# A second mixture of experts that adds its results into the output rows by scatter, in place of a table of results

## The chip, the cores and the metric

The kernel runs on one core of a Trainium2 chip. The metric is the device time of one execution in microseconds (us). The engines are PE (matrix products; PEld is its weight load), DVE (vector), ACT (scalar, activations), POOL (GpSimd) and SP (Sync). Each takes its instructions in program order. SP, ACT and POOL also issue DMAs; the indirect ones, which gather or scatter rows by a list of indices, are issued by POOL alone.

## The reference

Four layers act on `x`, 3125 rows of 256 numbers in fp32, with 50000 edges: a graph layer, a mixture of 8 experts (hidden size 1024), a second graph layer and a second mixture of 8 experts (hidden size 256). Each adds its result to `x`. The change is in the last:

```python
def _moe(tokens, router_w, w1, b1, w2, b2):
    logits = tokens.astype(jnp.float32) @ router_w.astype(jnp.float32).T
    probs = jax.nn.softmax(logits, axis=-1)
    rw, re = jax.lax.top_k(probs, TOP_K)                       # TOP_K = 2, 8 experts
    rw = rw / jnp.maximum(rw.sum(-1, keepdims=True), 1e-12)
    combine = jnp.zeros((N, E), tokens.dtype).at[jnp.arange(N)[:, None], re].set(rw)
    out = tokens
    for e in range(E):
        h = jax.nn.gelu(tokens @ w1[e] + b1[e], approximate=False)
        y = h @ w2[e] + b2[e]
        out = out + combine[:, e:e + 1] * y
    return out
...
x = x + _L1_ffn_ref(_layernorm(x, axis=-1)[None], ...)[0]
return x
```

So a row of the final output is `x`, plus its normed row (`out = tokens`), plus two weighted results of experts.

## The kernel before

`X` holds all rows in the on-chip memory, as 25 tiles of 128 rows (the last has 53). The tiles are split in two halves, 14 and 11 tiles (`HALVES`). In each mixture every expert gets a fixed room of places per half: 4 units of 128 places in the first half, 3 in the second (`UNITS`); tokens past that would go to extra sets, which a branch at the end runs only where they are needed.

The second graph layer runs in `to_the_end`. Its products (L1503) fill PE; `finish_tile` follows each tile, and at the end of every group of up to five tiles `score` norms the rows, adds the normed rows to `X` on POOL (`plus_normed`, L1421) and forms the router's logits. When the first half is complete, `route_steps` ranks the experts, gives every token two places (`r.at`) and two weights (`r.weight`), and calls `list_steps`, which turns the places around: for every place, which token to take (`take`) and which row of a result table to put the result into (`put`). It does that by one-hot products: `lane` and `col` are comparisons made on DVE, and PE multiplies them (L751) in parts of up to `r.part` tiles. A place that no token holds gets an index outside the table, and the scatter leaves it out. For the first half the rows themselves are sent to their places (`dispatch`, L1475), and the experts read them in blocks; for the second half POOL gathers the rows by `take` (L909).

`experts` then runs 16 sets, 8 experts for each half. Its order is written out by hand: instructions go to each engine in the order of the code. For one set PE does the first product (L949), ACT the activation into `hid` (L953), PE the transposes for the next set (`turn`, L925, copied by DVE at L926) and the second product, one unit of 128 places after the other (L962); DVE adds the bias (L967) and POOL scatters the unit into the half's result table `ytab` (L968), which was cleared to zeros far ahead, during the first mixture (`clear_steps`). `take` issues the gathers for later sets between these. The scatters of all sets go to different rows of a table, and `alone` declares that they need no order. Generators run beside the sets, one step in each `slot()`: `beside_third` makes the second half's lists, and `beside_fourth`, once all of the first half's sets are done, reads the first half's table back (`results`), adds the two weighted results of each row to `X` (`combine`, L998) and stores the rows to `out`. After the last set `combine_all` does the same for the second half.

Of the kernel before, what the change touches and what calls it, by code (L numbers as in the profile page):

```python
# [16 lines left out]
P = 128  # L17
D = 256
# [71 lines left out]
def gnn_ffn_kernel(ctx: ExitStack, tc: tile.TileContext, x, src_a, src_d, dst_d, dst_row,  # L90
# [134 lines left out]
    def clear(ytab):  # L225
        for _ in clear_steps(ytab):
            pass

    def tables(h, layer, by_place=False):

        rows = (FIXED[h] + XS * SX if by_place else HALVES[h][1] - HALVES[h][0]) * P
        return (dram.tile([rows, D], F32, name=f"xtab{layer}{h}{int(by_place)}"),
                dram.tile([2 * tokens(h), D], F32, name=f"ytab{layer}{h}{int(by_place)}"))
# [343 lines left out]
    class Routed:  # L577
# [4 lines left out]

        def __init__(self, by_place=False, part=T):
            self.by_place = by_place
            self.part = part
            self.done = False
            self.lists = {}
# [32 lines left out]
    def route_steps(r, rp, h, pl, layer, sc=None):  # L620
# [87 lines left out]
        yield from list_steps(r, rp, h, layer, 0, FIXED[h])  # L708
# [17 lines left out]
        r.weight_x = keep.tile([P, 2, n], F32, tag=f"weightx{layer}{h}", name="weight_x")  # L726
        nc.vector.scalar_tensor_tensor(r.weight_x, r.at, FIXED[h] * P - 0.5, r.weight, OP.is_gt, OP.mult)
        yield

    def list_steps(r, rp, h, layer, c0, c1):  # L730


        t0, t1 = HALVES[h]
        n = t1 - t0
        nl = c1 - c0
        ati = rp.tile([P, 2, n], I32, name="ati")
        nc.vector.tensor_copy(ati, r.at)
        qi = rp.tile([P, 2, n], I32, name="qi")
        nc.vector.tensor_scalar(qi, ati, P - 1, None, OP.bitwise_and)
        qb = rp.tile([P, 2, n, 2], BF16, name="qb")  # L740
        nc.vector.tensor_copy(qb, qi[:, :, :, None].to_broadcast([P, 2, n, 2]))
        nc.vector.tensor_scalar(qi, ati, 7, None, OP.arith_shift_right)
        cb = rp.tile([P, 2, n, 2], BF16, name="cb")
        nc.vector.tensor_scalar(cb, qi[:, :, :, None].to_broadcast([P, 2, n, 2]), -float(c0), None, OP.add)
        pt = bank([P, 2, nl], F32, "sa", 1)
        parts = [(i, a, b) for i in range(2) for a, b in groups(n, r.part)]
        made = []

        def count(i, a, b, lane, col):
            for t in range(a, b):  # L750
                nc.tensor.matmul(pt, lane[:, t - a, :], col[:, t - a], start=(i + t == 0), stop=(i + t == n))  # L751

        for i, a, b in parts:
            yield
            m = b - a
            lane = rp.tile([P, min(r.part, n), P], BF16, name="lane", bufs=2)
            nc.vector.tensor_tensor(in_pairs(lane[:, :m]), pairs(qb[:, i, a:b], P),
                                    in_pairs(iota_b[:, None, :].to_broadcast([P, m, P])), OP.is_equal)
            yield
            col = rp.tile([P, min(r.part, n), 2, nl], BF16, name="col", bufs=2)  # L760
            nc.vector.tensor_tensor(in_pairs(col[:, :m, 1, :]), pairs(cb[:, i, a:b], nl),
                                    in_pairs(iota_b[:, None, :nl].to_broadcast([P, m, nl])), OP.is_equal)
            nc.vector.tensor_tensor(in_pairs(col[:, :m, 0, :]), in_pairs(col[:, :m, 1, :]),
                                    tile1[:, a:b, None, :].to_broadcast([P, m, nl // 2, 2]), OP.mult)
            nc.vector.tensor_scalar(col[:, :m, 1, :], col[:, :m, 1, :], row2[:, i:i + 1], None, OP.mult)
            made.append((i, a, b, lane, col))
            if len(made) == 2:
                yield
                count(*made.pop(0))
        yield  # L770
        for one in made:
            count(*one)
            yield
        yield
        low = rp.tile([P, nl], F32, name="low")
        nc.vector.tensor_scalar(low, pt[:, 1, :], -float(2 * P), None, OP.add)
        which = rp.tile([P, nl], F32, name="which")
        nc.vector.scalar_tensor_tensor(which, pt[:, 0, :], float(2 * P), low, OP.mult, OP.add)
        put = keep.tile([P, nl], I32, tag=f"put{layer}{h}{c0}", name="put")
        take = keep.tile([P, nl], I32, tag=f"take{layer}{h}{c0}", name="take")  # L780
        whole = rp.tile([P, nl], I32, name="whole")
        nc.vector.tensor_scalar(whole, which, 0.0, None, OP.max)
        nc.vector.tensor_scalar(take, whole, 1, None, OP.arith_shift_right)
        none = rp.tile([P, nl], F32, name="no")
        nc.vector.tensor_scalar(none, pt[:, 0, :], 0.5, float(1 << 20), OP.is_lt, OP.mult)
        nc.vector.tensor_tensor(put, which, none, OP.max)
        r.lists[c0, c1] = (take, put)
        r.done = True
# [37 lines left out]
    def alone(dma, table, fresh=False):  # L826

        group = f"{table.name}{fresh}"
# [26 lines left out]
    def experts(fp, sets, routed, tabs, weights, nh, act, beside=(), fresh=False, early=0, loaded=None,  # L855
# [74 lines left out]
        with tc.manual_schedule(engines=ENGINES):  # L930
# [9 lines left out]
            for k, (h, e, x) in enumerate(sets):  # L940
# [16 lines left out]
                take(1)  # L957
                slot()
                for j in range(n):
                    py = bank([P, D], F32, "y")  # L960
                    for c in range(nh):
# [6 lines left out]
                    alone(nc.gpsimd.indirect_dma_start(  # L968
                        out=tabs[h][1], out_offset=bass.IndirectOffsetOnAxis(ap=routed[h].column(c0 + j)[1], axis=0),
                        in_=y, in_offset=None, bounds_check=2 * tokens(h) - 1, oob_is_err=False), tabs[h][1], fresh)  # L970
# [30 lines left out]
    def combine_all(fp, h, r, ytab, over, then=lambda t0, t1: None, bufs=2):  # L1001
        spans = groups(HALVES[h][1], 2, HALVES[h][0])
        ahead = []
        for i, (t0, t1) in enumerate(spans):
            while len(ahead) < min(bufs, len(spans) - i):
                ahead.append(results(fp, h, ytab, *spans[i + len(ahead)], bufs))
            y2 = ahead.pop(0)
            for t in range(t0, t1):
                combine(h, r.weight_x if over else r.weight, y2, t0, t)
            then(t0, t1)  # L1010

    def store(t0, t1):
        whole = min(t1, T - 1)
        if whole > t0:
            nc.sync.dma_start(out=out[t0 * P:whole * P, :].rearrange("(t p) d -> p t d", p=P),
                              in_=X[:, t0:whole, :])
        if t1 == T:
            nc.sync.dma_start(out=out[(T - 1) * P:, :], in_=X[:LAST, T - 1, :])
# [156 lines left out]
    with tc.tile_pool(name="ffn", bufs=2, reuse_waits="tile") as fp:  # L1175
# [134 lines left out]
        def beside_first():  # L1310
# [7 lines left out]
            with tc.tile_pool(name="onehots", bufs=2, reuse_waits="tile") as hp:  # L1318
                yield from total_in(hp, into)
                clears = [c for table in (tabs2[0][0], tabs2[0][1], tabs2[1][1]) for c in (clear_steps(table),)]  # L1320
                for i, _ in enumerate(count_edges(hp, 0, T)):
                    if i % 10 == 9 and clears and next(clears[0], 0) == 0:
                        clears.pop(0)
                    yield
                for c in clears:
                    for _ in c:
                        pass
# [94 lines left out]

    def to_the_end():


        routed2 = [Routed(True, 5), Routed()]
        with tc.tile_pool(name="ahead", bufs=6, side="right", reuse_waits="tile") as ap, \
# [18 lines left out]
            def finish_tile(sp, t, s):  # L1446
# [8 lines left out]
                if t == t1 - 1:  # L1455
                    unit(state["emb"], state["sq"], t0, t1)
                    h = int(t0 >= HALVES[1][0])
                    if t0 == HALVES[h][0]:
                        state["pl"] = bank([P, HALVES[h][1] - t0, NE], F32, "sb", 1)
                    score(sp, h, t0, t1, state["pl"], rWt, tabs2[h][0], plus_normed,  # L1460
                          state["kept"][:, t0:t1, :] if h == 0 else None, nc.scalar)
                    if h == 0 and t1 == HALVES[0][1]:
# [51 lines left out]
        with tc.tile_pool(name="ffn2", bufs=3, side="right", reuse_waits="tile") as fp:  # L1514
# [4 lines left out]
            def beside_fourth():  # L1519
                while now2[0] <= NE:  # L1520
                    yield
                with tc.tile_pool(name="behind", bufs=1, reuse_waits="tile") as zp:
                    spans = groups(HALVES[0][1], 2)
                    ahead = []
                    for i, (t0, t1) in enumerate(spans):
                        while len(ahead) < min(4, len(spans) - i):
                            ahead.append(results(zp, 0, tabs2[0][1], *spans[i + len(ahead)], 4))
                        if i == 0:
                            for _ in range(10):
                                yield  # L1530
                        y2 = ahead.pop(0)
                        for t in range(t0, t1):
                            combine(0, routed2[0].weight, y2, t0, t)
                            yield
                        store(t0, t1)
                        yield
                        yield

            now2 = [0]
            experts(fp, fixed(0) + fixed(1), routed2, tabs2, weights2, KD, AF.Gelu,  # L1540
                    [beside_third(), beside_fourth()], early=3, now=now2, room=24)
# [4 lines left out]
            with tc.tile_pool(name="last", bufs=1, reuse_waits="tile") as lp:  # L1546
                combine_all(lp, 1, routed2[1], tabs2[1][1], False, store, 6)
# [3 lines left out]
        with tc.If(more > 0):  # L1551
            with tc.tile_pool(name="ffn2", bufs=3, reuse_waits="tile") as fp:
                for h in range(2):
                    with tc.tile_pool(name="route4", bufs=1, reuse_waits="tile") as rp:
                        extra_sets(rp, h, routed2[h], 2)
                    experts(fp, extras_of(h), routed2, tabs2, weights2, KD, AF.Gelu, fresh=True)
                    combine_all(fp, h, routed2[h], tabs2[h][1], True, store)

    def to_the_end_by_edges():
# [162 lines left out]
        tabs2 = [tables(h, 2) for h in range(2)]  # L1722
        routed2 = []
        for h, (a, b) in enumerate(HALVES):
            with tc.tile_pool(name="score2", bufs=2, reuse_waits="tile") as sp, tc.tile_pool(name="route2", bufs=1, reuse_waits="tile") as rp:
                pl = bank([P, b - a, NE], F32, "sb", 1)
                for t0, t1 in groups(b, 5, a):
                    score(sp, h, t0, t1, pl, rWt, tabs2[h][0], plus_normed)
                routed2.append(route(rp, h, pl, 2))
                extra_sets(rp, h, routed2[h], 2)  # L1730
        with tc.tile_pool(name="ffn2", bufs=3, reuse_waits="tile") as fp:
            for h in range(2):
                clear(tabs2[h][1])
                experts(fp, fixed(h) + extras_of(h), routed2, tabs2, weights2, KD, AF.Gelu)
                combine_all(cp, h, routed2[h], tabs2[h][1], False, store)
# [59 lines left out]
```

## Time and profile before

| | |
|---|---|
| median of 14 runs | 1173.42 us (1169.17 to 1177.74) |
| the profiled execution | 1174.55 us, span 1172.8 us |
| PE busy | 1024.2 us (87%), PEld 765.1 us |
| DVE, ACT, POOL busy | 589.8, 323.6, 342.5 us |
| scatters into result tables (L968), both mixtures | 112, 1109 ns each on POOL |
| gathers of rows (L909), both mixtures | 80, 1019 ns each on POOL |
| weighting and adding results (L998), both mixtures | 100, 500 ns each on DVE |
| reads of result tables | 24 of 512 KB and 2 of 106 KB |

The times of the trace count from the span's start. The sets of the second mixture begin at about 998 us; the first graph layer, the first mixture and the second graph layer lie before. A row of a timeline gives the start, the time taken, the engine, the line with the operation, `out<-in`, and in brackets how long the engine was idle before it and what ended that.

### The profile page before, as it was taken

What the parts mean: (1) busy time and instruction counts of PE and PEld (TensorE: products, weight loads), DVE (VectorE), ACT (ScalarE), POOL (GpSimd) and SP (SyncE); (2) the same over time, 40 slices, a digit from 0 to 9 for tenths busy, and PEclk for the clock granted to TensorE, in tenths of its full rate; (3) what the DMA queues carried; (4) which work ended last, traced back from release to release, by engine and by line L of the source; (5) the groups of instructions that cost most, each with busy time, mean ns of one, the idle gap of its engine ahead of it and who ended that gap; (6) DMA issues with size and microseconds to landing.
All of it is one profiled execution on the core that took longest, in us unless ns stands there. A gap on an engine that the chain in (4) does not pass through costs nothing. (4 is left out here: it accounts for less than half of the span.)

```text
span 1172.8 us, 16050 instructions
## 1 busy us (share of the span) xinstructions
PE 1024.2 (87%) x6043; PEld 765.1 (65%) x6051; DVE 589.8 (50%) x1481; ACT 323.6 (28%) x709; POOL 342.5 (29%) x358
## 2 busy tenths in 40 slices
PE   6996455998999999999998999999999996877890
PEld 6984342666666677777666788888877785555660
DVE  9963383476365556565544162634371425722453
ACT  2362131121135555666432111121100112101110
POOL 1234506333332322222221111011122311366640
PEclk9787686999999999999998999999999996888895
DMA  7663254353247785786642170511122101754754
GB/s 211 222 175 106 77 185 122 120 174 109 86 112 250 269 281 206 273 295 211 216 159 94 68 272 3 225 56 57 57 88 69 50 28 58 223 163 143 259 188 158
DMA packets 116607, 179.41 MB, mean 153 GB/s; under 512 B 20204, under 2 KB 91237, under 8 KB 116393
## 3 DMA queue, kind: packets, MB, share of 16 engines
q1 hardware_dynamic: 94237, 120.40, 31.4%
q0 software_dynamic: 13296, 34.55, 9.0%
q10 hardware_dynamic: 8980, 23.26, 5.2%
q8 instruction: 51, 0.84, 0.3%
q14 instruction: 43, 0.35, 0.1%
HBM read 108.30 MB, written 71.76 MB: 154 GB/s over the span
## 5 line engine op out<-in xcount | busy, mean ns | idle before, releaser
L949 PE MATMUL big<-xs,w 128*128 128x512 f32 (+1 forms) x640 | 290.5, 580 | 15.9 <-ACT hid L953 13.4
L962 PE MATMUL y<-w,hid 128*128 128x256 f32 x1120 | 278.4, 394 | 17.8 <-ACT hid L953 10.1
L962 PEld LDWEIGHTS y<-w,hid 128*128 128x128 f32 x1120 | 207.1, 194 | 48.7 <-ACT hid L953 11.7
L1503 PEld LDWEIGHTS <-at 128*128 128x128 bf16 x1875 | 184.9, 99 | 29.8 <-DMA at<-atab 2.6
L968 POOL DMA_INDIRECT ytab<-y,put x112 | 124.2, 1109 | 228.8 <-DVE y L967 160.1
L953 ACT ACTIVATE hid<-big,bt 128x512 f32<-128x512 f32 (+1 forms) x160 | 101.6, 635 | 274.3 <-PE big L949 196.7
L949 PEld LDWEIGHTS big<-xs,w 128*128 128x128 f32 x640 | 116.7, 200 | 89.8 <-issue 43.8
L1503 PE MATMUL big<-parts,at 128*128 128x256 bf16 x1200 | 146.4, 275 | 2.1 <-DMA at<-atab 1.8
L909 POOL DMA_INDIRECT g<-xtab,take x80 | 81.5, 1019 | 174.3 <-PE tr L925 112.6
L967 DVE TENSOR_TENSOR y<-y,b2t 128x256 f32<-128x256 f32 x112 | 47.0, 423 | 135.6 <-PE y L962 112.3
L1160 PEld LDWEIGHTS <-hq 128*128 128x128 bf16 x800 | 57.2, 98 | 60.8 <-issue 40.4
L1140 DVE TENSOR_TENSOR hq<-qs,iota_b 128x2048 bf16<-128x2048 bf16 x50 | 61.1, 1222 | 54.0 <-PE sb L1160 46.1
L926 DVE COPY xs<-tr 128x512 f32<-128x512 f32 (+1 forms) x64 | 37.1, 619 | 74.6 <-PE tr L925 47.9
L998 DVE SCALAR_TENSOR_TENSOR X<-y,weight,X 128x256 f32<-128x256 f32 (+1 forms) x100 | 46.8, 500 | 46.6 <-DMA y<-ytab 45.6
L1503 PE MATMUL sa<-parts,at 128*128 128x256 bf16 x525 | 65.9, 277 | 1.6 <-issue 1.5
L1161 ACT CAST at<-sa 128x400 bf16<-128x400 f32 x100 | 49.1, 491 | 48.8 <-PE sa L1160 45.5
L1161 ACT CAST at<-sb 128x400 bf16<-128x400 f32 x100 | 49.1, 491 | 31.5 <-PE sb L1160 25.9
L1401 ACT COPY hT<-tr 128x512 f32<-128x512 f32 x25 | 14.4, 587 | 154.1 <-PE tr L1399 148.8
L1143 DVE TENSOR_TENSOR hc<-cs,iota_b 128x1600 bf16<-128x1600 bf16 x50 | 49.2, 985 | 0.0
L1421 POOL TENSOR_TENSOR X<-X,kept 128x256 f32<-128x256 f32 x14 | 10.4, 773 | 125.8 <-DVE kept L486 125.8
L519 PE MATMUL big<-gWo,hT 128*128 128x272 f32 x100 | 31.6, 456 | 16.6 <-remote 8.1
L417 PEld LDWEIGHTS <-hot 128*128 128x128 bf16 x391 | 40.6, 150 | 6.9 <-issue 3.8
(316 smaller groups left out, 1177.3 us busy)
## 6 DMA issues: line engine op xcount, KB each, us to landing
w<-in_fW SPq DMA_DIRECT2D x32, 1024.0 KB
atab<-at ACTq DMA_DIRECT2D x25, 800.0 KB
at<-atab SPq DMA_DIRECT2D x25, 800.0 KB
y<-ytab SPq DMA_DIRECT2D x24, 512.0 KB
ytab<-zero_b SPq DMA_DIRECT2D x10, 1024.0 KB
w<-in_mw SPq DMA_DIRECT2D x32, 256.0 KB
xtab<-zero_b SPq DMA_DIRECT2D x6, 1024.0 KB
rows<-xtab SPq DMA_DIRECT2D x8, 512.0 KB
```

The lines of the kernel that those rows point to most:

```text
L909: nc.gpsimd.indirect_dma_start(out=g, out_offset=None, in_=tabs[h][0], in_offset=bass.IndirectOffsetOnAxis(ap=routed[h].column(c)[0], axis=0))
L949: nc.tensor.matmul(ph[:, :n * P], w1[:, i, c * P:(c + 1) * P], turned[k][:, i, :n * P], start=(i == 0), stop=(i == KD - 1))
L953: nc.scalar.activation(hid[:, c, :n * P], ph[:, :n * P], act, bias=bt[:, 0, c:c + 1])
L962: nc.tensor.matmul(py, hid[:, c, j * P:(j + 1) * P], w2[:, c, :], start=(c == 0), stop=(c == nh - 1))
L967: nc.vector.tensor_add(y, py, b2t)
L968: alone(nc.gpsimd.indirect_dma_start(out=tabs[h][1], out_offset=bass.IndirectOffsetOnAxis(ap=routed[h].column(c0 + j)[1], axis=0), in_=y, ...
L998: nc.vector.scalar_tensor_tensor(X[:n, t, :], y2[:n, t - t0, i, :], weight[:n, i, i0:i0 + 1], X[:n, t, :], OP.mult, OP.add)
L1140: nc.vector.tensor_tensor(in_pairs(hq), pairs(qs[:, mine], P), in_pairs(iota_b[:, None, :].to_broadcast([P, n, P])), OP.is_equal)
L1143: nc.vector.tensor_tensor(in_pairs(hc), pairs(cs[:, mine], C), in_pairs(iota_b[:, None, :C].to_broadcast([P, n, C])), OP.is_equal)
L1160: nc.tensor.matmul(pa[:, j], hq[:, g + j, :], hc[:, g + j, :], start=True, stop=True)
L1161: nc.scalar.copy(at[:, :, W * (g0 + g):W * (g0 + g + 4)].rearrange("p i (g w) -> p i g w", w=W), pa.rearrange("p g i w -> p i g w"))
L1503: nc.tensor.matmul(sums[a][:, t - a, :], at[t][:, i, :], parts[:, i, k, :], start=False, stop=(i == T - 1 and k == 2 and t == b - 1))
```

## The change

The second mixture has no result table. Every tile of `X` is stored to `out` as soon as its normed rows have been added (`store` is called behind `score`, on ACT's queue). A unit's result is multiplied by the weights of its places on ACT and then scattered by an indirect DMA that adds to the rows of `out`. `list_steps` makes the weights by place: a weight is split in three bf16 parts, the one-hot columns are multiplied by each, and the same products sum them (`mine`). For this layer it therefore runs behind the weights in `route_steps`. A place that no token holds gets a row of the other half from an index fill (`spares`) and the weight 0, since the rows of one scatter have to differ. Scatters of one set are declared free of order among themselves, those of different sets no longer. `beside_fourth`, the last `combine_all` and the clears of two tables are gone; the first half's sets take one gather less each; the parts of the first half's list are 3 tiles long and not 5.

```diff
@@ route_steps
-        yield from list_steps(r, rp, h, layer, 0, FIXED[h])
+        if layer == 1:
+            yield from list_steps(r, rp, h, layer, 0, FIXED[h])
...
-        r.weight_x = keep.tile([P, 2, n], F32, tag=f"weightx{layer}{h}", name="weight_x")
-        nc.vector.scalar_tensor_tensor(r.weight_x, r.at, FIXED[h] * P - 0.5, r.weight, OP.is_gt, OP.mult)
+        if layer == 1:
+            r.weight_x = keep.tile([P, 2, n], F32, tag=f"weightx{h}", name="weight_x")
+            nc.vector.scalar_tensor_tensor(r.weight_x, r.at, FIXED[h] * P - 0.5, r.weight, OP.is_gt, OP.mult)
+        else:
+            yield from list_steps(r, rp, h, layer, 0, FIXED[h])
@@ list_steps
-        pt = bank([P, 2, nl], F32, "sa", 1)
+        kinds = 2 if layer == 1 else 5
+        if kinds > 2:
+            wb = rp.tile([P, 3, 2, n, 2], BF16, name="wb")
+            rest = r.weight
+            for k in range(3):
+                nc.vector.tensor_copy(wb[:, k], rest[:, :, :, None].to_broadcast([P, 2, n, 2]))
+                if k < 2:
+                    left = rp.tile([P, 2, n], F32, name="left", bufs=2)
+                    nc.vector.tensor_sub(left, rest, wb[:, k, :, :, 0])
+                    rest = left
+            yield
+        pt = bank([P, kinds, nl], F32, "sa", 1)
...
+            for k in range(2, kinds):
+                nc.vector.tensor_tensor(in_pairs(col[:, :m, k, :]), in_pairs(col[:, :m, 1, :]),
+                                        wb[:, k - 2, i, a:b, None, :].to_broadcast([P, m, nl // 2, 2]), OP.mult)
...
+            step = rp.tile([P, nl], F32, name="step")
+            spare = spares[h][:, c0:c1]
+            nc.vector.scalar_tensor_tensor(step, take, float(t0 * P), spare, OP.add, OP.subtract)
+            nc.vector.scalar_tensor_tensor(step, pt[:, 0, :], 0.5, step, OP.is_gt, OP.mult)
+            nc.vector.tensor_tensor(put, step, spare, OP.add)
+            mine = keep.tile([P, nl], F32, tag=f"mine{h}{c0}", name="mine")
+            nc.vector.tensor_reduce(mine, pt[:, 2:, :].rearrange("p k c -> p c k"), AX.X, OP.add)
+            r.lists[c0, c1] = (take, put, mine)
@@ experts
-                take(1)
+                if nh > 2 or h == 1:
+                    take(1)
...
-                    alone(nc.gpsimd.indirect_dma_start(
-                        out=tabs[h][1], out_offset=bass.IndirectOffsetOnAxis(ap=routed[h].column(c0 + j)[1], axis=0),
-                        in_=y, in_offset=None, bounds_check=2 * tokens(h) - 1, oob_is_err=False), tabs[h][1], fresh)
+                    to = routed[h].column(c0 + j)
+                    into = bass.IndirectOffsetOnAxis(ap=to[1], axis=0)
...
+                        nc.scalar.activation(y, y, AF.Identity, scale=to[2])
+                        alone(nc.gpsimd.indirect_dma_start(
+                            out=tabs[h][1], out_offset=into, in_=y, in_offset=None,
+                            bounds_check=N - 1, compute_op=OP.add), tabs[h][1], f"{h}{e}{x}")
@@ beside_first
-                clears = [c for table in (tabs2[0][0], tabs2[0][1], tabs2[1][1]) for c in (clear_steps(table),)]
+                clears = clear_steps(tabs2[0][0])
@@ to_the_end
+    spares = []
+
+    def spare_rows():
...
+            nc.gpsimd.iota(each[:, :FIXED[h]].rearrange("p (e u) -> p e u", e=NE), pattern=[[0, NE], [P, UNITS[h]]],
+                           base=base, channel_multiplier=1)
...
-        routed2 = [Routed(True, 5), Routed()]
+        routed2 = [Routed(True, 3), Routed()]
+        spare_rows()
...
                     score(sp, h, t0, t1, state["pl"], rWt, tabs2[h][0], plus_normed,
                           state["kept"][:, t0:t1, :] if h == 0 else None, nc.scalar)
+                    store(t0, t1, nc.scalar)
...
-            def beside_fourth():
...
             experts(fp, fixed(0) + fixed(1), routed2, tabs2, weights2, KD, AF.Gelu,
-                    [beside_third(), beside_fourth()], early=3, now=now2, room=24)
+                    [beside_third()], early=3, room=24)
...
-            with tc.tile_pool(name="last", bufs=1, reuse_waits="tile") as lp:
-                combine_all(lp, 1, routed2[1], tabs2[1][1], False, store, 6)
```

## The prediction

> **What bounds the kernel now.** I read the page first (engine rows, clock row, chain), then the chain of waits at its end, then tables by stage and the timelines of PE, POOL and DVE from 990 us on, and last the two built programs' orders. The page's second part says that PE is nearly full everywhere but at the start and in the last tenth:
>
> ```profile
> PE   6996455998999999999998999999999996877890
> ```
>
> The last zero is the stage that the change deletes. By stage (busy us of PE, PEld, DVE, ACT, POOL; then the granted clock, DMA share and GB/s):
>
> ```profile
> 1130.00:1145.00 15.00, 13.12 (x55) 9.42 (x53) 4.85 (x11) 2.33 (x4) 7.93 (x9) 1.00 0.15 57
> 1145.00:1173.00 28.00, 0.00 (x0) 0.00 (x0) 9.14 (x22) 0.00 (x0) 0.95 (x1) 0.52 0.49 160
> ```
>
> For 28 us no matmul runs. The chain of waits shows what does:
>
> ```profile
> 1144.96 2.31 DMA ytab<-y,put
> 1147.28 0.37 SPq L985
> 1147.70 2.64 SPq L985
> 1152.09 10.54 DMA y<-ytab
> 1162.72 0.49 DVE X L998
> ```
>
> The last scatter takes 2.31 us from issue to landing; then the second half's results are read back, combined (L998) and stored, and the span ends at 1172.8. From that landing to the end it is 25.5 us. The other engine that matters is POOL, which issues every scatter (L968) and gather (L909) in program order (start, us, tile):
>
> ```profile
> 1083.95 1.01 POOL L968 DMA_INDIRECT ytab<-y,put  x1 [4.85 <-DVE y L967]
> 1085.66 1.00 POOL L968 DMA_INDIRECT ytab<-y,put  x1 [0.69 <-DVE y L967]
> 1086.97 0.99 POOL L909 DMA_INDIRECT g<-xtab,take  x1 [0.30 <-issue]
> 1088.26 1.01 POOL L968 DMA_INDIRECT ytab<-y,put  x1 [0.30 <-issue]
> 1089.57 0.99 POOL L968 DMA_INDIRECT ytab<-y,put  x1 [0.30 <-issue]
> ...
> 1127.70 0.99 POOL L968 DMA_INDIRECT ytab<-y,put  x1 [0.30 <-issue]
> 1130.87 0.98 POOL L968 DMA_INDIRECT ytab<-y,put  x1 [2.18 <-DVE y L967]
> 1132.16 0.99 POOL L968 DMA_INDIRECT ytab<-y,put  x1 [0.30 <-issue]
> 1133.45 0.98 POOL L968 DMA_INDIRECT ytab<-y,put  x1 [0.30 <-issue]
> ```
>
> Back to back they come every 1.3 us; towards the end POOL waits for PE, whose period per expert of the second half is 5.83 us:
>
> ```profile
> 1125.87 2.74 PE L949 MATMUL big<-xs,w 128*128 128x384 f32 x8
> 1131.70 2.74 PE L949 MATMUL big<-xs,w 128*128 128x384 f32 x8
> ```
>
> **The tail goes.** Of the 25.5 us, the reads, combines and stores leave. What stays is leaving the program. The trace's own records on POOL behind the landing are 0.3 us of semaphore waits, a queue step of 1.5, a branch with 2.9 to the next instruction and a drain of 5.4, to 1157.4; the closing handshake takes 0.9 more. That is 11.0 us after the landing, hidden today behind the stores. On SP the same exit takes 5.1 us from the last store's landing (1167.7). A gain of 14.5 to 20.4; I take 14.5, since POOL's instructions are unchanged.
>
> **The new wait.** Scatters of one expert go unordered among themselves, but the first scatter of an expert now waits until all of the expert before have landed, because they add to the same rows. The built order puts that wait on POOL; queued behind it are the expert's other scatters and the gathers, and PE waits for those. The price depends on two numbers that no row shows: c, from one scatter-add to the next on POOL, and L, from issue to landing. A plain scatter has c = 1.3 and L = 2.3 in a quiet stretch; around 1096 to 1112, beside the 512 KB loads, the landing events come 5 to 6 us after issue. An addition also reads what it adds to; a gather, which reads HBM, lands at some 2.5. I take c = 1.4 and L = 3.3, nearer the quiet rows since those loads are gone; the bounds are c 1.3 to 2.0, L 2.3 to 5.0. Below today's values nothing can fall: a read is added.
>
> The Trainium skill bears on this ("Collectives: The Full Stack", section "The bandwidth ceiling: the fold count and why AG ≠ RS ≠ AR"): adding inside the DMA emits two reads for each piece and halves the rate. No row here shows an addition. An estimate from it doubles the 1.32 us between the end of the issue (0.99) and the landing (2.31): L would be 3.6, and the sum below 2.4 us more.
>
> First half, four scatters and two gathers an expert (three gathers before): 1.4+1.4+1.3+1.4 up to the fourth, then 3.3+0.2 for landing and wake-up: 9.0 us. PE's period there was (1088.12-1021.02)/6 = 11.2, because fp32 matmuls ran slowly in parts of it (DVE takes the y of 1036 to 1041 us 2.1 us apart, those of 1130 to 1132 0.86). POOL keeps up. Second half, scatter, scatter, gather, scatter, gather: 4.1 to the third scatter, then 3.5: 7.6, against PE's 5.83. So POOL paces it. The eighth expert's first scatter starts at 1083.95 plus 0.6 for the scaling on ACT (below), 1084.6; its others and the gathers follow at 1086.3, 1087.7 (gather), 1089.0, 1090.4, 1091.8 and 1093.1 (gathers), so the ninth's starts at 1094.4, the fourteenth's at 1094.4+5x7.6 = 1132.4. That expert's gather, the 24th and last, starts at 1135.2; before, the last gather left at 1111.3. PE needs it for the sixteenth expert's transposes (2.5 us to land, 0.8 for them) and does them ahead of y of the fifteenth: its first scatter is ready at 1135.2+2.5+0.8+0.9+1.0 = 1140.4 (landings allow 1140.0), its third starts at 1143.2, the sixteenth's first at 1146.7 (landing; PE, with 2.8 and 2.7 us of matmuls, 0.6 for the activation and 1.9 to the first scaled y, is ready at 1146.5), its third at 1149.5; landed 1152.8. Against 1147.3 that is 5.5 later. The loss: +5.5.
>
> The combines beside the second half also leave (28 of the 50 at L998, on DVE from 1103 to 1123.6, where PE stood 3.19 and 1.68 us). I count no gain: PE would only wait for POOL.
>
> **The scaling.** 56 activations of 128x256 move onto ACT, which was busy 24.6 of 188 us. The nearest row, same shape:
>
> ```profile
> 988.13 0.42 ACT L1409 ACTIVATE junk<-emb 128x256 f32<-128x256 f32 x1 [4.85 <-DVE emb L1407]
> ```
>
> They lie beside PE, ahead of the next expert's first activation, which needs 1.4 us of matmuls; only the 0.6 us hop to the scatter counts, once, and is in the chain above.
>
> **Lists and stores.** For the first half, 10 parts of 7 DVE operations replace 6 parts of 4, which stood from 866.2 to 874 us. From start to start a part of three tiles takes 0.3 for the 384-column comparison and six times 0.14 for the small products (rows of the same kind on the DVE timeline): 1.1 us, and 0.7 for splitting the weights: 12 us for 8. DVE then stood idle 8.08 us to 883.30, which covers it; without that cover the 4 us would fall on PE. PE pays for 28 matmuls of 160 columns, not 64: 0.04 us each more (a 256-column one takes 0.11), about 1 us; none to 3 with waits. For the second half the weights come ahead of the list and six products are added; the matmuls that need the list move from the second expert's y into the third's first product. Following DVE's order, the list's columns are ready at some 1024.5, the third expert's first product ends 1025.9 and not 1024.5: +1.4 (0 to 3). Stores of X go onto ACT's queue behind POOL's additions; only the last stands in the way, 0.4 us ahead of the copy at 992.33. The clears (6.4 MB) leave SP in a stretch where PE is full: nothing. Four index fills on POOL lie ahead of 693 us, where it idles from 673.8. Together +2.8 (0 to 6).
>
> **Clock.** PE will stand some us for the last gather. Around stands at 1042 to 1046 and 1075 to 1080 the granted clock was halved for 7 us from 1047 and for 10 from 1078; after one of 1.7 us at 1117 it was not. Nothing to 5 us; I put +1, since PE's own slow parts may close the gap.
>
> **Sum.** -14.5 + 5.5 + 2.8 + 1.0 = -5.2. The profiled execution took 1174.55 (span 1172.8 and 1.75 around it), 1.1 above the median of 1173.42. So 1169.3 in its terms, 1168.2 beside the median. 0.2%, 2.3 us, is about what can be told from no change.
>
> **Rivals.** (1) Slower: additions land late. Each us on L costs about 8 us (five periods, three steps at the end), so 0.65 us more than I take, L = 3.95, eats the gain. With L = 5.0 the ninth's first scatter is at 1095.6, the period 9.3, the landing 1167.2: +19.9-14.5+3.8 = +9.2, time 1182.6; with c = 2.0 as well some +25. For it: landings of 5 to 6 us when queues were full. Against: they were full of loads that go. Chance 0.32, with every slower end. (2) Additions land as plain scatters do, L = 2.4 and c = 1.3: period 6.5, last landing 1145.1; -2.2-14.5+2.8 = -13.9, 1159.5. For it: the packets of a scatter span only 0.4 us of its landing. Chance 0.21. (3) No change: L near 4, or PE at half clock for its last two experts (+5): 1173, chance 0.11. That the change doesn't do what it says is excluded but for the exit: were POOL's drain shorter without the stores, 6 us more would go; that lies within (2).
>
> **Numbers.** My case: 0.36. Faster 0.36+0.21 = 0.57, within 0.2% 0.11, slower 0.32. The range runs from 1158 (rival 2 with a little of the exit) to 1187 (rival 1 past L = 5); the doubled issue cost lies beyond.
>
> **What would show it.** No DMA to or from a result table after 1000 us, none between the last scatter and the end; 11 us from that landing to the end; first scatters of experts 9 to 14 idle until a scatter landed, 7.6 us apart; the last gather near 1135; scatter-adds of 1.0 to 1.1 us on POOL landing at 3.3. The prediction is wrong if the landing is past 4 us, if POOL's time per scatter-add is past 1.5, if the first half too runs at POOL's pace, or if the end comes 5 us after the last landing.

## The result, and the profile after: slower by 2 per cent

The changed kernel took 1199.28 us (median of 10 runs, 1188.64 to 1207.49), the kernel before 1172.56 beside it. The ratio is 1.0197, with a 95% interval of 1.0172 to 1.0222. The profiled execution took 1198.87 us, its span 1197.0, which is 24.2 more than the 1172.8 of before.

The PE row of the page, 40 slices of the span, answers to the one shown of before; the POOL row stands with it:

```profile
PE   6986537998999999999998999999988997896553
POOL 2244415432542112322321120110121410666763
```

The empty last slice of before is gone, but in the last four PE is busy for only six to three tenths, and in five of the last six POOL is busy for six to seven. The table by stage shows both (busy us of PE, PEld, DVE, ACT, POOL; granted clock, DMA share, GB/s):

```profile
1040.00:1080.00 40.00, 40.00 (x164) 27.29 (x163) 14.05 (x29) 16.51 (x29) 26.54 (x20) 1.00 0.78 162
1080.00:1145.00 65.00, 37.80 (x125) 27.27 (x124) 12.19 (x26) 13.11 (x26) 45.17 (x35) 0.76 0.64 118
1145.00:1185.00 40.00, 23.16 (x73) 16.09 (x71) 6.48 (x14) 8.93 (x17) 25.14 (x19) 0.79 0.48 71
1185.00:1197.00 12.00, 0.00 (x0) 0.00 (x0) 0.00 (x0) 0.00 (x0) 1.32 (x1) 0.50 0.22 28
```

From 1040 to 1080 PE never stops; behind that PE works for little more than half the time, and then only 12 us are left in place of 28. What PE stands for is in the waits of PE from 1040 us on (total us, times, longest):

```profile
PE tr L953 <- DMA g<-xtab,take: 36.2, 10, 7.9
```

It stands 36.2 us for gathered rows. The gathers are late because POOL issues them late. This is POOL's timeline for one expert of the second half and the start of the next (start, us):

```profile
1142.67 1.57 POOL L1006 DMA_INDIRECT out<-y,put  x1 [1.62 <-DMA out<-y,put]
1144.55 1.56 POOL L1006 DMA_INDIRECT out<-y,put  x1 [0.31 <-issue]
1146.41 1.01 POOL L937 DMA_INDIRECT g<-xtab,take  x1 [0.30 <-issue]
1147.73 1.57 POOL L1006 DMA_INDIRECT out<-y,put  x1 [0.30 <-issue]
1149.61 1.01 POOL L937 DMA_INDIRECT g<-xtab,take  x1 [0.30 <-issue]
1152.44 1.57 POOL L1006 DMA_INDIRECT out<-y,put  x1 [1.82 <-DMA out<-y,put]
```

A scatter that adds holds POOL for 1.57 us, and the next instruction starts 1.87 behind it, not 1.3. The next expert's first scatter stands until this expert's additions have landed: 4.7 us behind the start of the last of them. From expert to expert that is 9.8 us, where PE's products need 5.83. The group on the page says the same of all 56 (in before, 1109 ns is the mean of the 112 scatters of both mixtures):

```profile
L1006 POOL DMA_INDIRECT out<-y,put x56 | 87.6, 1565 | 67.8 <-ACT y L1005 20.8
```

The end, from the timeline of POOL: the last scatter leaves at 1184.77, and by the trace's semaphore events its data has landed at 1189.09. The span ends 7.9 us behind that:

```profile
1184.77 1.55 POOL L1006 DMA_INDIRECT out<-y,put  x1 [0.30 <-issue]
```

A ledger of the two spans has three entries. The sets begin at 1005.59 and not 998.15: +7.4. From there to the last landing it takes 183.5 us and not 149.1: +34.4. From the landing to the end 7.9 and not 25.5: -17.6. The sum is +24.2.

### The profile page after: what moved, and what is told of

Same layout as the page of the kernel before. It is cut to its first block, busy times and chain, and to the rows that moved or that the text cites. A ratio compares the mean times of both kernels' runs of the same rounds, so it can differ in the third digit from the quotient of the medians.

```text
span 1197.0 us, 16119 instructions
## 1 busy us (share of the span) xinstructions
PE 1033.8 (86%) x6043; PEld 774.1 (65%) x6051; DVE 580.7 (49%) x1495; ACT 349.7 (29%) x765; POOL 374.4 (31%) x362
## 5 line engine op out<-in xcount | busy, mean ns | idle before, releaser
L977 PE MATMUL big<-xs,w 128*128 128x512 f32 (+1 forms) x640 | 290.5, 579 | 16.3 <-ACT hid L981 13.7
L991 PEld LDWEIGHTS y<-w,hid 128*128 128x128 f32 x1120 | 211.9, 198 | 37.8 <-DVE y L996 6.8
L1551 PE MATMUL big<-parts,at 128*128 128x256 bf16 x1200 | 151.0, 279 | 2.1 <-DMA at<-atab 1.7
L1000 POOL DMA_INDIRECT ytab<-y,put x56 | 67.3, 1202 | 163.2 <-DVE y L996 122.2
L1006 POOL DMA_INDIRECT out<-y,put x56 | 87.6, 1565 | 67.8 <-ACT y L1005 20.8
L953 PE MATMUL tr<-ident,g 128*128 128x128 f32 x160 | 28.8, 313 | 43.3 <-DMA g<-xtab,take 43.3
L1005 ACT ACTIVATE y<-y,mine 128x256 f32<-128x256 f32 x56 | 28.4, 508 | 103.6 <-DVE y L996 97.9
L953 PEld LDWEIGHTS tr<-ident,g 128*128 128x128 f32 x160 | 21.4, 159 | 53.9 <-DMA g<-xtab,take 47.3
```

The lines of the kernel that those rows point to most:

```text
L953: nc.tensor.transpose(px[:, j, :], taken[k][j][:, i * P:(i + 1) * P], ident)
L977: nc.tensor.matmul(ph[:, :n * P], w1[:, i, c * P:(c + 1) * P], turned[k][:, i, :n * P], start=(i == 0), stop=(i == KD - 1))
L991: nc.tensor.matmul(py, hid[:, c, j * P:(j + 1) * P], w2[:, c, :], start=(c == 0), stop=(c == nh - 1))
L1000: alone(nc.gpsimd.indirect_dma_start(out=tabs[h][1], out_offset=into, in_=y, in_offset=None, bounds_check=2 * tokens(h) - 1, oob_is_err=Fa ...
L1006: alone(nc.gpsimd.indirect_dma_start(out=tabs[h][1], out_offset=into, in_=y, in_offset=None, bounds_check=N - 1, compute_op=OP.add), tabs[ ...
L1551: nc.tensor.matmul(sums[a][:, t - a, :], at[t][:, i, :], parts[:, i, k, :], start=False, stop=(i == T - 1 and k == 2 and t == b - 1))
```

## The experiments

Each was timed against the kernel before on the same chip. The chips differ: before took 1173.4 us beside the first four kernels, 1163.9 beside the next four, 1107.8 beside the three after those and 1166.8 beside the last. So ratios are compared within a group only; a difference between ratios of two groups is a hint. A second measure leaves out all that lies ahead of the sets: the time from the begin of the sets to the last landing, or to the end, in the profiled execution. Before and no_tail (below), which have the same sets, take 149.1 and 146.2 us to the last landing, on two chips, so some 3 us of it can be chance.

### Is it the addition, or the order between sets?

**plain**, the changed kernel with scatters that overwrite:

```diff
-                            bounds_check=N - 1, compute_op=OP.add), tabs[h][1], f"{h}{e}{x}")
+                            bounds_check=N - 1), tabs[h][1], f"{h}{e}{x}")
```

> The changed kernel with plain scatters in place of scatters that add (so a row keeps only the last result sent to it); order, waits, scaling and lists are unchanged. Theory A, the price lies in the addition: POOL goes back to 1.3 us from one scatter to the next and landings to about 2.4, so a set of the first half takes POOL 1.3 x 3 to the fourth scatter plus 2.4 plus 0.8 of waits = 7.1 us, below PE's own 7.8, and a set of the second half 7.1 in place of 9.7: some 35 to 45 us off, 1155 to 1165 us. Theory B, the price is the order between sets whatever is sent: more than three quarters of the time stays, 1185 to 1199 us.

It took 1172.88 us, 0.9976 of before (0.9941 to 1.0011). The changed kernel's sibling **skip** (below), which adds, took 1197.12 on the same chip, so with this order the addition costs 24 us. POOL's group on its page:

```profile
L1006 POOL DMA_INDIRECT out<-y,put x56 | 55.6, 993 | 69.2 <-ACT y L1005 33.4
```

993 ns in place of 1565. In quiet stretches the trace's semaphore events show the plain scatter landed 2.2 to 2.4 us after its start, the adding one 3.7 to 3.8. Theory A's size was missed, though: it expected 1155 to 1165. Its first half was not at PE's 7.8 us a set: the starts of the sets there lie 7.8 to 14.0 us apart (in before 8.0 to 16.9), and from 1080 to 1090 us the granted clock is 0.83. Theory B, the order alone, falls. But the rest of the change is not free either: plain has lost the tail, which by no_tail is worth 12 us, and is hardly faster than before.

**table_add**, the kernel before with scatters that add into the cleared table:

```diff
-                        in_=y, in_offset=None, bounds_check=2 * tokens(h) - 1, oob_is_err=False), tabs[h][1], fresh)
+                        in_=y, in_offset=None, bounds_check=2 * tokens(h) - 1, oob_is_err=False,
+                        **({"compute_op": OP.add} if nh == 2 else {})), tabs[h][1], fresh)
```

> The kernel before with nothing changed but that its scatters of the second mixture add to the rows of the cleared result table; no order between sets, tail as before. Theory A, an addition costs 1.87 us from one to the next on POOL but hurts only together with the wait for landings: POOL's work of a set is 4 x 1.87 + 3 x 1.32 = 11.4 us in the first half beside PE's 11.2, and 5.6 in the second beside PE's 5.83, and the last landing comes 1.5 us later: 1174 to 1180 us. Theory C, additions are slow by themselves wherever they go: 15 us or more on top, above 1187 us.

It took 1175.94 us, 1.0038 of before (1.0009 to 1.0068): theory A. Its page has 1394 ns as the mean of both mixtures' scatters (1109 before), and from 1085 us on POOL issues without a gap. PE's longest stand, 19.2 of 23.5 us, is for DVE, which has no buffer for `y`, since POOL has not sent those that are full:

```profile
1103.61 2.07 PE L962 MATMUL y<-w,hid 128*128 128x256 f32 x4 [19.17 <-DVE y L967]
```

Yet the last scatter left 150.4 us behind the begin of the sets (994.87 to 1145.26), where before it left 146.8 us behind it. Without an order between the sets, POOL's longer issue nearly fits into the time that it had free. From the begin of the sets to the last landing it is 149.1 us in before, 155.3 in plain, 155.7 in table_add and 183.5 in after. So the order (in plain, with the scaling and the longer list of the second half) and the addition (in table_add) cost some 6 us each alone; together they cost 34.

**skip**, the changed kernel where a place without a token gets an index past the end:

```diff
-            nc.vector.scalar_tensor_tensor(step, take, float(t0 * P), spare, OP.add, OP.subtract)
-            nc.vector.scalar_tensor_tensor(step, pt[:, 0, :], 0.5, step, OP.is_gt, OP.mult)
-            nc.vector.tensor_tensor(put, step, spare, OP.add)
+            nc.vector.tensor_scalar(step, pt[:, 0, :], 0.5, float(1 << 20), OP.is_lt, OP.mult)
+            nc.vector.scalar_tensor_tensor(put, take, float(t0 * P), step, OP.add, OP.max)
...
-                            bounds_check=N - 1, compute_op=OP.add), tabs[h][1], f"{h}{e}{x}")
+                            bounds_check=N - 1, oob_is_err=False, compute_op=OP.add), tabs[h][1], f"{h}{e}{x}")
```

> The changed kernel where a place without a token gets an index past the end of the output, which the scatter leaves out, in place of a spare row and the weight 0. 12.5 per cent of the first half's places and 13 of the second's hold no token. If POOL's 1.55 us of a scatter that adds go by its rows, it falls to about 1.36 and the time by some 8 us, to 1191; if they go by instruction, both stay (1199, within 3).

1197.12 us, and 1566 ns a scatter: POOL's time goes by instruction, not by the rows that are sent.

### Where does the wait lie?

**mixed3**, from skip: another order of the sets, and scatters of different halves free of order:

```diff
+            a, b = fixed(0), fixed(1)
+            mixed = a[:3] + [s for p in zip(b, a[3:]) for s in p] + b[5:]
-            experts(fp, fixed(0) + fixed(1), routed2, tabs2, weights2, KD, AF.Gelu,
+            experts(fp, mixed, routed2, tabs2, weights2, KD, AF.Gelu,
...
+        tc.declare_no_dep(dma.ins, group=f"half{1 - h}", reason="rows of the other half")
+        tc.add_to_no_dep_group(f"half{h}", dma.ins)
```

> The kernel skip with another order of the 16 sets: three of the first half, then five pairs of one set of the second half and one of the first, then the last three of the second; scatters of different halves, whose rows differ, are declared free of order. Theory A, the time is lost where POOL stands for a landing between two sets of one half: in the pairs that wait lies behind the other set's scatters and POOL runs through, 7 x 1.87 + 3 x 1.32 = 17.1 us a pair in place of 12.7 + 9.7 = 22.4; five pairs give 27 us, 1170 us in all (1164 to 1180). Theory B2, POOL's issue alone is what counts, not the landing: the pairs bring nothing, 1190 to 1199.

It took 1171.1 us, 1.0064 of before (1.0036 to 1.0093). The changed kernel was not run in this group; its own ratio elsewhere is 1.0197. Theory A's times were meant for the chip of skip, where they are 0.997 of before (0.992 to 1.006) and theory B2's 1.014 or more: B2 falls, and theory A's gain came out smaller than it said. From the begin of the sets to the end skip takes 190.1 us and mixed3 174.7, so 15 of the 27 us are won; before takes 174.7 as well. POOL runs through between the sets of a pair; here is the step from one half to the other and back, in mixed3:

```profile
1088.94 1.57 POOL L1009 DMA_INDIRECT out<-y,put  x1 [0.30 <-issue]
1090.82 1.56 POOL L1009 DMA_INDIRECT out<-y,put  x1 [0.30 <-issue]
...
1095.86 1.57 POOL L1009 DMA_INDIRECT out<-y,put  x1 [0.30 <-ACT hid L984]
1097.73 1.56 POOL L1009 DMA_INDIRECT out<-y,put  x1 [0.30 <-issue]
...
1102.19 1.61 POOL L1009 DMA_INDIRECT out<-y,put  x1 [0.30 <-issue]
```

No gap in the pairs is longer than 0.31 us. A pair took 18.4 us (four gathers, not the three expected) in place of 22.4. What is left in the pairs is POOL's issue itself; ahead of the last two sets it still stands 2.9 and 5.8 us.

**mixed4**, the same with four sets ahead and four behind:

> As mixed3, but four sets of the first half first, four pairs, and four sets of the second half at the end. Theory A: one pair fewer, 5 us more than mixed3, 1175 us (1169 to 1185). Theory B2: 1190 to 1199.

1178.03 us (1.0120; 1.0086 to 1.0154), 7 above mixed3 on the same chip, where theory A expected 5; from the begin of the sets to the end it is 180.1 us, 5.4 more than in mixed3. So a pair less and a waiting set more cost about what the landing wait costs.

### The late start

**lists**, the kernel before with the list part of the change (the edits at `route_steps` and `list_steps` in the diff above, parts of three tiles, the weights by place made and not used):

> The kernel before with the list part of the change alone: the lists of the second mixture behind the weights, with five kinds of columns in place of two and parts of three tiles in the first half; the weights by place are made and not used. The prediction put this at +2.4 us (1175); by the trace of after, where the sets begin 7.4 us later, it is +5 to +9 (1178 to 1182).

1175.84 us, 1.0032 of before (1.0002 to 1.0063): 2.5 us by the medians, as the prediction put it, but the interval runs to 7.4. The traces tell more. The list lies between the products of one tile (L1404 of before, L1436 of after) and those of the next:

```profile
865.27 1.13 PE L1404 MATMUL y<-hW1t,hT 128*128 128x256 f32 x4
885.39 1.13 PE L1404 MATMUL y<-hW1t,hT 128*128 128x256 f32 x4
861.44 1.13 PE L1436 MATMUL y<-hW1t,hT 128*128 128x256 f32 x4
890.00 1.13 PE L1436 MATMUL y<-hW1t,hT 128*128 128x256 f32 x4
```

The first two lines are of before, 20.1 us apart, the others of after, 28.6 apart; in plain and skip it is 28.7 and 28.6, in lists 23.4. So the longer list takes some 3 us there, and 5 more are lost. The waits of PE from 855 to 945 us in after name them, and so does its clock:

```profile
PE sa L765 <- DVE col L782: 3.1, 1, 3.1
PE sa L765 <- DVE col L775: 2.4, 1, 2.4
...
PE sa L765 <- PE big L1551: 0.6, 1, 0.6
```

```profile
870.00:875.00 5.00, 1.02 (x9) 0.89 (x10) 2.11 (x13) 0.00 (x0) 3.40 (x4) 0.93 0.19 79
875.00:880.00 5.00, 3.91 (x22) 2.98 (x22) 3.43 (x21) 0.00 (x0) 0.00 (x0) 0.50 0.08 31
```

In the list PE and DVE wait in turn for each other, while POOL issues eight dispatches from 863.9 to 874.8 without a pause; behind the stand the granted clock is 0.50. In before the second four of those dispatches left at 874.0 us, when the list was nearly done, since the copy of their indices (L1472) ran at 873.6 on DVE; now that copy (L1520) runs at 867.7, among the first columns of the list.

**later** puts the second four behind it again:

```diff
-                            first = 2 * (t - HALVES[1][0])
+                            first = 2 * (t - HALVES[1][0] - 1)
```

> The changed kernel with the dispatches of the first half's rows begun one tile later, so that POOL issues the second eight DMAs behind the list and not in its midst. Theory D, the 7.4 us by which the sets begin late come from PE's stands of 2.4 and 3.1 us in the list, while POOL issues dispatches, and from the half clock behind them; the longer list itself costs the 2 us seen with the lists alone: the sets begin 4 to 6 us earlier, 1193 to 1195 us. Theory E, the longer list makes the delay whatever POOL does: the sets begin at 1004 to 1006 us, 1197 to 1201.

1182.39 us, 1.0157 of before (1.0108 to 1.0206), against the changed kernel's 1.0197 elsewhere; the two intervals touch, so the time alone does not settle it. The trace does: the same stretches in later have

```profile
870.00:875.00 5.00, 4.64 (x43) 3.70 (x43) 4.60 (x31) 0.00 (x0) 0.00 (x0) 1.00 0.08 31
875.00:880.00 5.00, 4.95 (x46) 4.06 (x45) 3.96 (x26) 0.00 (x0) 0.00 (x0) 1.00 0.00 0
```

PE's waits in the list add up to 1.7 us and not 6.1, with the same list, and the stretch of 28.6 us is 22.4 long. The sets begin at 990.12; in mixed3 and mixed4, which have the dispatches in the midst of the list and ran on the same chip, they begin at 996.27 and 994.46. That is 4 to 6 us, as theory D had it. Why the hand-over between PE and DVE was late while POOL issued is open.

### The tail

**no_tail**, the kernel before without its last `combine_all` (these rows are not stored):

> The kernel before without the last reading, weighting and storing of the second half (these rows of the output are left out). The prediction's price of the tail: 11.0 us from the last landing to the end in place of 25.5, so 14.5 us off, 1158.5 us. By the changed kernel's exit (7.9 us from landing to end): 17.6 off, 1155.5.

1151.54 us, 0.9896 of before (0.9867 to 0.9924), so 12.1 us (8.8 to 15.5) off: the prediction's 14.5 lies within, the 17.6 of after does not. In its trace 11.0 us pass from the last landing to the end, POOL's drain being 5.44 us as in before. In after the drain took 3.25 us and the queue step 0.95 in place of 1.49. plain has 5.46 and 1.50, table_add 3.24 and 0.94. But it does not go with the kind of the last scatter: the hybrids below end with scatters that add, and have drains of 5.44 to 5.52 and steps of 1.49 to 1.51. The short exit is that of the kernels in which all 56 scatters of the mixture add; no run shows why.

### Towards a kernel that beats both

**hybrid3** is the kernel before with three edits: only the second half's results are scaled and added into `out`, with weights by place for that half alone; the sets stand as in mixed3; the first half's table is read back and weighted beside the last sets of the second half. **hybrid4** stands as mixed4. **mixed3_later** joins mixed3 and later.

```diff
+                    if nh > 2 or h == 0:
...
+                    else:
+                        nc.scalar.activation(y, y, AF.Identity, scale=to[2])
+                        put = nc.gpsimd.indirect_dma_start(
+                            out=tabs[h][1], out_offset=into, in_=y, in_offset=None,
+                            bounds_check=N - 1, oob_is_err=False, compute_op=OP.add)
...
-                while now2[0] <= NE:
+                while now2[0] <= 12:
```

> The kernel before, but only the second half's results are added into the output by scatter (with weights by place for that half alone; the first half keeps its result table, its list and its weighting beside the products), and the 16 sets stand as in mixed3: three of the first half, five pairs, three of the second half. Theory A: a landing of the second half's additions lies behind the first half's plain scatters, POOL needs 4 x 1.3 + 3 x 1.87 + 4 x 1.3 = 16 us a pair in place of 18.4, the first half's list and the sets' begin are those of before, and no result is read back behind the last set: 5 x 2.4 + 5 = 17 us below mixed3 and some 10 below before (0.985 to 0.997 of it). Theory F, the landings and the hole that PE has where the second half's list comes late eat it: 1.000 or above.

> As hybrid3, with four sets of the first half ahead, four pairs and four sets of the second half at the end, each of which waits for the one before (9.7 us each in place of PE's 5.8). Theory A: the fourth set gives POOL time for the gathers, the fourth waiting set costs 4 us: within 4 us of hybrid3, 0.985 to 1.000 of before.

> mixed3 and the later dispatches together: if the two losses are apart, 4 us below mixed3, 1.002 to 1.004 of before; if the delay of the list was hidden behind POOL's queue in mixed3, no change, 1.006.

They took 1122.66 us (1.0113 of before; 1.0077 to 1.0150), 1126.56 (1.0172; 1.0141 to 1.0203) and 1131.79 (1.0205; 1.0177 to 1.0233). Theory A missed for both hybrids. For mixed3_later nothing follows from the total, since mixed3 was not run on this chip, where before needs 56 us less than on the one of mixed3. From the begin of its sets to the end it takes 174.7 us, as mixed3 does, so the mixed order is worth the same here; what it loses against before on this chip is not explained, since no profile of before was taken there. hybrid3 takes 168.6 us from the begin of the sets to the end, 6.1 less than mixed3 in place of the 17 expected. The waits of PE in hybrid3 from 1065 us on show where some of the gain went:

```profile
PE y L994 <- ACT hid L985: 13.9, 2, 13.7
```

and DVE's timeline shows what was behind it:

```profile
1087.54 1.00 DVE L1040 SCALAR_TENSOR_TENSOR X<-y,weight,X 128x256 f32<-128x256 f32 x2 [15.33 <-DMA y<-ytab]
```

DVE stood 15.3 us for the first rows of the result table; ACT's scaling stood behind DVE, and the next set's activation behind that scaling. **hybrid3_last** puts the weighting behind all sets on DVE:

```diff
-                            for _ in range(8):
+                            for _ in range(60):
...
-                        yield
```

> hybrid3 with the weighting of the first half's results behind the last set's bias additions on DVE, and not among them. In hybrid3 PE stood 13.7 us for ACT, ACT for DVE, and DVE for the reading of the result table. Theory A: that stand goes, the last three sets run at the landings' pace, the 14 us of weighting lie beside the last scatters: 8 to 10 us off, 1.002 to 1.006 of before. If the weighting then lies behind the last landing: no gain, 1.011.

It took 1162.8 us, 0.9967 of before (0.9945 to 0.9990), on a chip where before takes 1166.8: 4 us faster than before. The stand of 13.7 us is gone (0.2 us left in that stretch). Whether that made it faster is not shown: from the begin of the sets to the end it takes 170.3 us, in an execution 5.7 us above its median, and hybrid3 took 168.6; hybrid3 was not run on this chip. It is the one kernel of the study with the full output and a ratio below 1, and by little.

## Why the prediction was wrong

Rival 1 came true in its extreme form ("with c = 2.0 as well some +25"; the profiled execution is 24.3 us longer). That the number fits so well is partly luck: with c = 2.0 and L = 5.0 the period would be 10.5 us; it was 9.8, with c = 1.87 and L = 3.8, and 6.0 us of the loss lie ahead of the sets, where the rival had nothing. Against the predicted span of 1167.6 the real one has 29.4 us more:

| stretch | predicted | after | difference |
|---|---|---|---|
| begin of the sets | +1.4 | +7.4 | +6.0 |
| begin to the ninth expert's first scatter | 98.7 | 107.4 | +8.7 |
| ninth's to fourteenth's first scatter | 38.0 | 49.1 | +11.1 |
| from there to the last landing | 20.4 | 27.1 | +6.7 |
| landing to end | 11.0 | 7.9 | -3.1 |

(98.7 is the prediction's 1094.4 less 998.15, with the 2.4 that it put on the second half's list and the clock.)

- **The term that failed is the period on POOL, and in it first of all c.** For the second half the sum was 7.6 us; it is 9.8. Of the 2.2, c gives 1.0 (two scatters that add at 1.87 in place of 1.4), the landing 0.5 (3.8 in place of 3.3), the wake-up 0.7 (from landing to the next start 0.9 in place of 0.2: POOL goes through two semaphore waits and its set-up first). c was taken "nearer the quiet rows", but those rows were all plain DMAs, and a row of another kind is no measure for this one. Its bound of 2.0 was in the text, and the range still ended at 1187: it took L's bound in and left c's out. How much of the 29.4 us hangs on these terms, plain shows: it has the c = 1.3 and, in quiet stretches, the L = 2.4 of rival 2, and its span is 1171.3 in place of the 1158.9 that this rival's sum gives. So 12.4 us would have been missed with c and L right (5.5 in the begin, 6.9 in the sets), and 17.0 are the addition's.
- **"POOL keeps up" in the first half is wrong twice.** POOL needs 12.7 us there and not 9.0: 6.9 to the start of the fourth scatter in place of 5.5, then 5.8 to the next expert's first in place of 3.5, since that scatter lands 4.8 to 5.0 us after its start here, beside the weight loads (the DMA share is 0.78 from 1040 to 1080). And PE's own period there is not 11.2 but 7.76, at a granted clock of 1.00:

```profile
1047.30 3.60 PE L977 MATMUL big<-xs,w 128*128 128x512 f32 x8
1055.06 3.60 PE L977 MATMUL big<-xs,w 128*128 128x512 f32 x8
1062.83 3.60 PE L977 MATMUL big<-xs,w 128*128 128x512 f32 x8
```

  So POOL fell behind from the third expert on, out of sight, until PE first stood at 1081.5 and, from 1090.6, for gathered rows. The 11.2 of before was not all slow matmuls either, as the prediction had it: the results of 1036 to 1041 us came 2.1 us apart although the granted clock was 1.00 from 1030 to 1040, and from 1000 us on PE stood 10.1 us for ACT. Why it does not stand so in after is open.
- **The list was priced about right (lists: +2.5 us by the medians, 0.2 to 7.4 by the interval, against 2.4), its neighbour was not.** The prediction looked at DVE's free time behind the list and not at the dispatches on POOL, which the move of the list brought into its midst.
- **The tail was right in kind and in size** (10.9 us from landing to end in plain, 11.0 in no_tail). In after it was 7.9, to the good; "POOL's instructions are unchanged" did not hold there, though it did in the hybrids (10.9 to 11.1).
- **Right as well:** the wait at an expert's first scatter, with the gathers behind it; PE's stand for the gathers; no table read or written behind 1000 us. Two of its own signs of being wrong came: 1.57 us of POOL for a scatter that adds, and a first half at POOL's pace.
- **The rule of the Trainium skill** ("Collectives: The Full Stack", section "The bandwidth ceiling: the fold count and why AG ≠ RS ≠ AR") that an addition inside the DMA doubles its reads gave the estimate L = 3.6. The runs show 3.7 to 3.8 in quiet stretches, against 2.2 to 2.4 without the addition, so the estimate was nearer than the 3.3 taken. Its reason is not shown, though: 0.6 of the 1.45 us is POOL's own issue, of which that section says nothing, and the profile counts no second read. These are the rows of POOL's DMA queue (packets, MB) in before and in table_add, which differ in the addition alone:

```profile
q0 software_dynamic: 13296, 34.55, 9.0%
q0 software_dynamic: 18672, 34.56, 12.2%
```

  The bytes are the same, and so are the 108.30 MB read from HBM; the packets are 96 more for each of the 56 scatters.

## What to carry to other kernels

A wait costs its latency times the number of times that the queue behind it has nothing else to do: give that queue independent work between the two ends (from the begin of the sets to the end the mixed order won back 15 us; the order and the addition cost some 6 us each alone and 34 together). Price an operation that the profile doesn't show by its worst bound if it lies on a serial chain of 16 steps, and let the range hold all the bounds together. And when a step moves, look at what else is queued where it lands: here DMAs on POOL, in hybrid3 one wait on DVE that stopped three engines.

## What the hardware showed that was not expected

- An indirect scatter of 128 rows of 1 KB that adds holds POOL for 1.55 to 1.57 us in most rows, a plain one for 0.98 to 1.00, into the output and into a table alike, and no less with some 13 per cent of its rows left out. By the packet records the plain one moves as 32 packets of 4096 bytes and the one that adds as 128 of 1024.
- POOL's exit is shorter where all 56 scatters of the last mixture add: drain 3.25 against 5.44 us, queue step 0.95 against 1.49; with 24 of 56 it is not. No run shows why.
- The same program took 1107.8 us on one chip and 1173.4 on another; a ratio from one chip need not hold on the other. In mixed3_later the sets began 39.7 us earlier than in mixed3, on another chip, and took the same 174.7 us to the end.
